# Attention probabilities turned in place, an output bank per unit, and a new order of the work

## The chip, the cores and the metric

The kernel runs on one core of a Trainium2 chip. The metric is the device time of one execution in microseconds (us). Three runs of the kernel before gave 2599.71 us as their median (2597.64 to 2602.36). About 0.2% of that, some 5 us, is what a measurement of this kernel can tell from no change.

Engines are named as the profile names them: PE (the matrix engine; PEld its weight loads), DVE, ACT and POOL (the three others that compute), SP (which issues the DMAs). PE's results land in PSUM, which has eight banks of 512 fp32 columns; everything else lies in SBUF, on 128 partitions.

## What is computed

One encoder layer over a short context (2 batches, 77 tokens, 512 features) and one decoder layer over x (2 batches, 2048 tokens), all in fp32. The decoder layer attends causally to itself, then to the encoder's output, and ends in a feed-forward network of width 2048:

```python
causal = jnp.where(jnp.arange(Tt)[None, :] > jnp.arange(Tt)[:, None], -jnp.inf, 0.0)
sb = _rel_bias(dec_rel_self, Tt, Tt) + causal[None]
y = tgt
yn = _ln(y, dec_n1_s, dec_n1_b)
y = y + _mha(yn, yn, dec_sa_in_w, dec_sa_in_b, dec_sa_out_w, dec_sa_out_b, sb)
y = y + _mha(_ln(y, dec_n2_s, dec_n2_b), memory, ...)
h = _ln(y, dec_n3_s, dec_n3_b)
y = y + (jax.nn.relu(h @ dec_ff1_w.T + dec_ff1_b) @ dec_ff2_w.T + dec_ff2_b)
```

with, inside `_mha` (16 heads of 32 features):

```python
scores = jnp.einsum('bhqd,bhkd->bhqk', q, k) / jnp.sqrt(hd) + bias[None]
attn = jax.nn.softmax(scores, axis=-1)
out = jnp.einsum('bhqk,bhkd->bhqd', attn, v)
```

## The kernel before

**The self-attention in units.** It is cut into 128 units. A unit (b, m, g, t) is one batch, one block of 128 queries (the t-th of four in the m-th of four blocks of 512 tokens) and one group g of four heads. It has `size = 4*m + t + 1` blocks of 128 keys, from 1 to 16. A unit goes through four steps:

- `scores`: for up to four key blocks at a time, four matmuls (one per head, 32 rows of the array each) into four banks. DVE brings the banks into `pp` while it takes their maximum; the last two key blocks get the bias and the causal mask on the way.
- the exps: one ACT instruction per head over all of the unit's key blocks, in place in `pp`, with the row's sum beside it.
- `turn`: for two key blocks at a time, 16 transposes of 64 rows each into two banks, and two copies of 512 columns out of them, by ACT or DVE, into `pts`.
- `values`: per key block four matmuls (32 columns of the array each) that take the turned blocks and add up in one bank.

**Places before.** `pp` has two halves, one for even and one for odd units. `pts` holds eight turned blocks and is handed out as a pool (`turned_places`). The bank of `values` is held by the four units t of one (b, m, g) and copied out once, 512 columns wide, after the fourth.

**Tile shapes on PE.** The steps use the array in four shapes (rows x columns): 64x128 for the turns, 128x32 for the values and the projections of q, k, v and of the output, 32x128 for the scores, 128x128 for the feed-forward network. The names in the trace tell them apart: `psum<-ident,pp` is a turn, `psum<-pts,vv` values, `psum<-kT,q` scores, `psum<-nT,wqk`, `psum<-wbig,nT` and `psum<-wbig,oT` projections. The trace shows each fp32 matmul as two instructions, and a transpose as one.

**What sets the order.** The program's operations are first recorded (`Tape`) as tasks, with the tasks that each depends on. `Tape.plan` then sets the order by walking through time with its own estimates of durations: each task has a key (the unit's number plus an offset by kind), and a table `PLAN` gives, for every four units, the offsets, how far PE may run ahead of the lowest open key (`window`), and how much a task is preferred that keeps PE's tile shape (`stay`). A task starts only where its banks and places are free. It also decides whether ACT or DVE makes a copy. Every engine then runs its instructions in that fixed order and waits on semaphores. SP's queue of DMAs is in the same order.

**Around it.** The encoder is computed in between the first units. In the middle of the attention POOL prepares sums of the weights of the feed-forward network (`w2_sums`, `w2_store`, `w1_sums`, `w1_store`), which go to DRAM (`w_d` in the trace). From 1544 us on the cross-attention and the feed-forward network run. Every recorded instruction carries the line of the recorder, L457 of the profile, so groups are told apart by their tiles.

Of the kernel before, what the change touches and what calls it, by code (L numbers as in the profile page):

```python
# [12 lines left out]
F32 = mybir.dt.float32  # L13
# [58 lines left out]
def phase_of(window, hold, flex, stay, first, wide, look, pause, weights):  # L72
# [744 lines left out]
def tile_encoder_decoder(ctx: ExitStack, tc: tile.TileContext, ins, out):  # L817
# [102 lines left out]
    with (  # L920
# [205 lines left out]
        def probabilities(n):  # L1126
            w = (units[n][1] + 1) * MB
            at = END - HC * w if n % 2 else 0
            return [pp[:, at + r * w : at + (r + 1) * w] for r in range(HC)]
# [1360 lines left out]
```

## Time and profile before

| | before |
|---|---|
| runs | 2602.36, 2597.64, 2599.71 us |
| profiled execution, first to last instruction | 2600.6 us; the profile gives no other time for it, and it lies among the three runs |
| PE busy | 2574.9 us |
| self-attention: up to the last `values` | 1544 us; PE busy 1524.86, DVE 1217.09, ACT 1097.99 |
| cross-attention and feed-forward: the rest | 1057 us; PE busy 1050.01, DVE 601.20, ACT 413.20 |
| granted clock of PE, mean | 0.998 |

How to read it: "busy" is the time in which at least one instruction of an engine is under way. Matmuls overlap in PE's pipeline, so a row of n equal matmuls takes far less than n times the duration of one. In the timeline, the start of a row to the start of the next is what the row cost.

### The profile page before, as it was taken

To read this page: it belongs to the slowest core of one execution; us is meant where nothing else is said; L and a number is where in the kernel's file an instruction comes from. 1 tells how busy PE (TensorE), PEld (TensorE's weight loads), DVE (VectorE), ACT (ScalarE), POOL (GpSimd) and SP (SyncE) were. 2 spreads that over 40 slices of the span, in tenths; PEclk is the share of its full clock that TensorE was granted. 3 is DMA by queue.
4 is the path that set the end of the run, shared out by engine and by line. 5 is a ranking of instruction groups with operands and counts; after the bars stand their busy time and mean duration, and the time that the engine had idled before them with its cause. 6 is when DMAs were issued, how large, how long until landed. Compare 5 with 4: busy or idle time off the path is not lost.

```text
span 2600.6 us, 84216 instructions
## 1 busy us (share of the span) xinstructions
PE 2574.9 (99%) x35494; PEld 1803.0 (69%) x35494; DVE 1818.3 (70%) x5243; ACT 1511.2 (58%) x2898; POOL 823.9 (32%) x757
## 2 busy tenths in 40 slices
PE   9999999999999999999999999999999999999999
PEld 4556555555555455555555677989898989999998
DVE  5766688788887787888788874747474746474744
ACT  4665578777877576678787874433425353434431
POOL 1200152000001011202000023938474757566546
PEclk9999999999999999999999999999999999999999
DMA  8323383111116222513112043646556655554566
GB/s 222 119 79 108 108 243 109 51 43 30 50 33 153 81 63 67 160 55 128 31 47 63 29 148 113 183 139 190 159 171 175 181 158 170 171 161 153 159 199 223
DMA packets 252716, 320.32 MB, mean 123 GB/s; under 512 B 29568, under 2 KB 142512, under 8 KB 252210
## 3 DMA queue, kind: packets, MB, share of 16 engines
q1 hardware_dynamic: 252338, 314.93, 40.7%
q8 instruction: 279, 4.57, 0.7%
q14 instruction: 99, 0.81, 0.1%
HBM read 274.91 MB, written 39.95 MB: 121 GB/s over the span
## 4 chain that ended last, share of the span: by engine, by line
PE 64%; ACT 1%; DVE 1%; issue 1%; DMA 0%; POOL 0%; POOLq 0%; ACTq 0%; DVEq 0%
PE psum L457 64%; ACT pp L457 0%; DVE pp L457 0%; ACT pts L457 0%; DMA pp<-w_d 0%; DVE pts L457 0%; DVE nT L457 0%; ACT nT L457 0%; DVE bnst L457 0%; POOLq L2486 0%; POOL vv L457 0%; DVE oT L457 0%; POOL crs L457 0%; ACT xt L457 0%; DVE vv L457 0%
## 5 line engine op out<-in xcount | busy, mean ns | idle before, releaser
L457 ACT ACTIVATE pp<-pp,nm 128x128 f32<-128x128 f32 (+15 forms) x512 | 612.9, 1204 | 141.0 <-DVE nm L457 140.5
L457 DVE TENSOR_SCALAR_CACHE_REDUCE pp<-psum 128x512 f32<-128x512 f32 (+3 forms) x1024 | 561.7, 590 | 124.2 <-PE psum L457 118.7
L457 ACT COPY pts<-psum 128x512 f32<-128x512 f32 (+2 forms) x789 | 404.6, 575 | 229.9 <-PE psum L457 191.4
L457 PEld LDWEIGHTS psum<-ident,pp 64*128 64x128 f32 (+1 forms) x8904 | 314.9, 139 | 182.7 <-issue 63.1
L457 PE MATMUL psum<-ident,pp 64*128 64x64 f32 (+1 forms) x8904 | 367.4, 227 | 5.8 <-DVE kT L457 1.5
L457 PE MATMUL psum<-pp 128*128 128x128 f32 (+4 forms) x3012 | 359.3, 281 | 0.3 <-DMA pp<-w_d 0.3
L457 PEld LDWEIGHTS psum<-pp 128*128 128x128 f32 (+3 forms) x3012 | 341.2, 189 | 15.6 <-DVE nm L457 1.6
L457 POOL TENSOR_TENSOR pp<-pp 128x512 f32<-128x512 f32 (+2 forms) x203 | 278.8, 1385 | 198.1 <-DVE pp L457 98.2
L457 PE MATMUL psum<-kT,q 32*128 32x512 f32 (+3 forms) x2560 | 334.4, 575 | 1.3 <-ACT nT L457 1.0
L457 DVE COPY pts<-psum 128x512 f32<-128x512 f32 (+2 forms) x475 | 288.5, 646 | 54.1 <-PE psum L457 51.0
L457 PE MATMUL psum<-pts,vv 128*32 128x128 f32 x8704 | 314.7, 276 | 4.7 <-ACT nT L457 2.8
L457 PEld LDWEIGHTS psum<-pts,vv 128*32 128x32 f32 x8704 | 220.9, 109 | 104.5 <-issue 70.2
L457 PE MATMUL psum<-vv,pp 128*128 128x256 f32 (+1 forms) x1072 | 254.1, 390 | 0.0
L457 PE MATMUL psum<-nT,wqk 128*32 128x512 f32 x2048 | 240.2, 595 | 2.5 <-DMA wqk<-in_dec_sa_in_wT_dram 1.3
L457 PEld LDWEIGHTS psum<-vv,pp 128*128 128x128 f32 (+1 forms) x1072 | 199.4, 188 | 39.3 <-issue 11.3
L457 DVE CUSTOM_DVE_ANT_0 pp<-psum,bias 128x256 f32<-128x256 f32 (+1 forms) x512 | 196.5, 411 | 25.7 <-PE psum L457 21.0
L457 DVE TENSOR_TENSOR oT<-psum,oT 128x256 f32<-128x256 f32 (+2 forms) x260 | 108.0, 425 | 122.7 <-PE psum L457 107.8
L457 PEld LDWEIGHTS psum<-kT,q 32*128 32x128 f32 x2560 | 108.3, 183 | 111.3 <-issue 45.2
L457 POOL TENSOR_TENSOR rstd<-rstd,mhalf 128x1 f32<-128x1 f32 x32 | 18.4, 576 | 506.5 <-DVE rstd L457 476.2
L457 PE MATMUL psum<-nT,pp 128*128 128x256 f32 x768 | 177.1, 382 | 0.0
L457 DVE TENSOR_TENSOR kT<-kT,psum 128x512 f32<-128x512 f32 x96 | 65.2, 682 | 139.4 <-PE psum L457 136.6
L457 PEld LDWEIGHTS psum<-nT,pp 128*128 128x128 f32 x768 | 143.6, 190 | 20.1 <-issue 0.6
(152 smaller groups left out, 3215.2 us busy)
## 6 DMA issues: line engine op xcount, KB each, us to landing
pp<-w_d SPq DMA_DIRECT2D x520, 256.0 KB, 2.9
pp<-in_dec_ff_wT_dram SPq DMA_DIRECT2D x112, 256.0 KB, 2.9
wqk<-in_dec_sa_in_wT_dram SPq DMA_DIRECT2D x64, 256.0 KB, 2.9
bias<-tzg SPq DMA_DIRECT2D x128, 128.0 KB, 3.3
wbig<-in_dec_sa_in_wT_dram SPq DMA_DIRECT2D x8, 1024.0 KB, 7.3
vv<-in_enc_ff_wT_dram SPq DMA_DIRECT2D x8, 1024.0 KB, 5.6
wbig<-in_dec_sa_out_wT_dram SPq DMA_DIRECT2D x8, 1024.0 KB, 5.9
vv<-y SPq DMA_DIRECT2D x32, 256.0 KB, 3.9
```

The lines of the kernel that those rows point to most:

```text
L457: getattr(getattr(self.nc, engine), op)(*map(real, a), **{n: real(v) for n, v in k.items()})
```

## The change

- **In place.** `pts` and its pool are gone. `pp` becomes a ring of 40 blocks, each a key block with its four heads side by side (2048 columns of one head per row become a step of 512 from key block to key block). A table `spots` gives each unit its blocks: fixed places for m = 0, 1, 2 and a ring for m = 3, where a unit may lie in two parts. `turn` copies the turned blocks back over the blocks that it read.
- **The exps** of a unit in two parts are two instructions per head, and a small DVE addition joins their sums.
- **An output bank per unit.** `values` takes a bank for each unit and copies it out, 128 columns wide, at the unit's end.
- **Other places.** What the cross-attention kept in `pts` is now at the end of `pp` (`tail`). The sums for the feed-forward network's second weights use the rear of `kT` and `vv`; their stores to DRAM are cut in another way (56 in place of 44).
- **New order.** Most of the attention's rows of `PLAN` have other numbers, and the order comes out otherwise. The matmuls and transposes are the same in number and shape.

```diff
@@ PLAN, one of 37 rows
-    (6.9, 2.5, 323, (0.463, 0.15, 0.337, 0.322), (-2.08, -0.5, 0, 1.75, -0.98, 0.33, -0.6, -0.5, -0.14, 0.42, -0.28),
+    (8.717, 1.874, 18, (0.835, 0.643, 0.759, 0.291), (-2.73, 0.328, 0, 0.919, 0.22, -0.017, -1.211, -1.071, -0.585, -0.499, -1.449),
...
-        pp = ac.tile([P, 2 * HC * T], F32, name="pp")
+        RING = 40
+        pp = ac.tile([P, RING * HC * P], F32, name="pp")
         END = 2 * HC * T
+        blocks_of_p = pp.rearrange("p (k r q) -> p k r q", r=HC, q=P)
...
-        pts_all = ac.tile([P, 8, HC * P], F32, name="pts")
...
-        banks, turned_places = Places(psum), Places(pts_all)
+        banks = Places(psum)
...
         def probabilities(n):
-            w = (units[n][1] + 1) * MB
-            at = END - HC * w if n % 2 else 0
-            return [pp[:, at + r * w : at + (r + 1) * w] for r in range(HC)]
+            size = units[n][1] * TB + units[n][3] + 1
+            at, first = spots[n]
+            parts = [(0, at, first)] + ([(first, 0, size - first)] if first < size else [])
+            return [(k, blocks_of_p[:, at : at + n]) for k, at, n in parts]
...
+        PLACES = ((0, 28, 32, 36), (0, 32, 24), (28, 0, 16))
...
+        for b, m, g, t in units:
+            size = m * TB + t + 1
+            if m < NMB - 1:
+                spot, at = (PLACES[m][(g * TB + t) % len(PLACES[m])], size), 0
+            else:
+                first = min(size, (RING - at) // TB * TB)
+                spot = (at, first) if first else (0, size)
+                at = sum(spot) if spot[1] == size else size - first
...
-                def run(p=p, nm=nm, to=to):
-                    nc.scalar.activation(p, p, AF.Exp, bias=nm, accum_out=to)
+                def run(r=r, nm=nm, to=to):
+                    parts = st["p"]
+                    for x, (_, p) in enumerate(parts):
+                        p = p[:, :, r]
+                        if x:
+                            to = st["more"][:, r : r + 1]
+                        nc.scalar.activation(p, p, AF.Exp, bias=nm, accum_out=to)
+                    if r == HC - 1 and len(parts) > 1:
+                        to = sums_of[b, m, g][:, t]
+                        nc.vector.tensor_tensor(to, to, st["more"], ALU.add)
...
         def turn(n, k0, kn):
-            pts = turned_places.take(kn)
+            place = part_of_p(n, k0, kn).rearrange("p k r q -> p (k r) q")
             two = [bank(), bank()]
...
-                        nc.tensor.transpose(two[a][:, ts(x, HALF)], src[at], ident[at, at])
...
+                        nc.tensor.transpose(two[a][:, ts(x, HALF)], place[rows, x], ident[rows, rows])
+            for a in range(2):
+                src = two[a][:, : HC * kn * HALF]
+                copy(place[:, :, ts(a, HALF)], src.rearrange("p (x q) -> p x q", q=HALF))
...
         def values(n, k0, kn):
...
-            if (b, m, g) not in held:
-                held[b, m, g] = bank()
...
+            if n not in held:
+                held[n] = bank()
+            if t == 0 and k0 == 0:
+                ots[b, m, g] = in_turn("oT", oT_all)
+            ot = held[n][:, :P]
...
-            if t == TB - 1 and k == i:
-                o = ots[b, m, g] = in_turn("oT", oT_all)
-                copy(o, got_bank)
+            if k == i:
+                copy(ots[b, m, g][:, ts(t, P)], ot)
...
-        for c, k in enumerate((0, 2, 4, 10)):
-            light[u + k + 2].append(lambda c=c: w2_store(c, 1))
-            late[u + k + 1].append(lambda c=c: w2_store(c, 0))
-        for c, k in enumerate((0, 2, 4, 10)):
+        for c, k in enumerate((0, 3, 6, 9)):
             light[u + k].append(lambda c=c: w2_sums(c))
+            for i, zs in enumerate(ranges):
+                light[u + k + 1 + i].append(lambda c=c, zs=zs: w2_store(c, *zs))
...
-        for t in nc.tasks[mark_loads:]:
-            if any(s.places is turned_places for s in t.slots):
-                t.before.add(behind)
```

**How the order moves.** Below, a row is a stretch of equal instructions on one engine; "x16" is their number in the program. Counted over all of PE's rows, the tile shape changes 1323 times before and 990 times after. Stretches without a change of shape go from 399 to 214 for the turns' shape (64x128), from 480 to 384 for that of the values and projections (128x32), from 349 to 297 for that of the scores (32x128), and stay at 96 for 128x128. The longest stretch of transposes goes from 80 to 152; stretches of more than 80 go from none to 42.

PE, the end of the second batch's attention, before: from the last unit's last scores (`kT,q`) to the first of its turns (`ident,pp`), with values (`pts,vv`), turns of the unit ahead and an output projection (`wbig,oT`) between them.

```order
L457 MATMUL psum<-kT,q_132 128x512 x4
L457 MATMUL psum<-ident,pp 128x64 x64
L457 MATMUL psum<-pts,vv 32x128 x16
L457 MATMUL psum<-ident,pp 128x64 x32
L457 MATMUL psum<-pts,vv 32x128 x16
L457 MATMUL psum<-ident,pp 128x64 x24
L457 MATMUL psum<-pts,vv 32x128 x16
L457 MATMUL psum<-wbig,oT 32x512 x8
L457 MATMUL psum<-pts,vv 32x128 x12
L457 MATMUL psum<-ident,pp 128x64 x64
```

PE, the same place after (the values now read `pp`).

```order
L457 MATMUL psum<-kT,q_131 128x512 x4
L457 MATMUL psum<-pp,vv 32x128 x16
L457 MATMUL psum<-wbig,oT 32x512 x16
L457 MATMUL psum<-ident,pp 128x64 x48
L457 MATMUL psum<-pp,vv 32x128 x8
L457 MATMUL psum<-ident,pp 128x64 x32
L457 MATMUL psum<-pp,vv 32x128 x8
L457 MATMUL psum<-ident,pp 128x64 x16
L457 MATMUL psum<-pp,vv 32x128 x8
L457 MATMUL psum<-ident,pp 128x64 x24
L457 MATMUL psum<-pp,vv 32x128 x36
L457 MATMUL psum<-ident,pp 128x64 x128
```

The last unit's 128 transposes, which stood in three pieces with values between them, now stand in one; other work stands between its last scores and its first turn as before, in another mixture.

PE, some units earlier in the same block of queries, before: turns, values and scores alternate.

```order
L457 MATMUL psum<-ident,pp 128x64 x16
L457 MATMUL psum<-kT,q_132 128x512 x4
L457 MATMUL psum<-ident,pp 128x64 x16
L457 MATMUL psum<-pts,vv 32x128 x16
L457 MATMUL psum<-ident,pp 128x64 x32
L457 MATMUL psum<-kT,q_132 128x256 x4
L457 MATMUL psum<-pts,vv 32x128 x8
L457 MATMUL psum<-ident,pp 128x64 x16
L457 MATMUL psum<-kT,q_132 128x512 x4
```

PE, there after.

```order
L457 MATMUL psum<-kT,q_131 128x256 x4
L457 MATMUL psum<-pp,vv 32x128 x4
L457 MATMUL psum<-ident,pp 128x64 x128
L457 MATMUL psum<-kT,q_131 128x512 x4
L457 MATMUL psum<-pp,vv 32x128 x32
L457 MATMUL psum<-kT,q_131 128x512 x4
L457 MATMUL psum<-pp,vv 32x128 x16
L457 MATMUL psum<-kT,q_131 128x512 x4
L457 MATMUL psum<-pp,vv 32x128 x16
```

All turns of a unit now stand in one stretch, and its scores and values alternate without turns between them.

ACT, the last units, before: exps (`pp,sums<-pp,nm`) and copies of turned blocks (`pts<-psum`).

```order
L457 COPY pts<-psum 128x8x64 x2
L457 ACTIVATE pp,sums_145<-pp,nm_139 128x1792
L457 COPY pts<-psum 128x8x64 x8
L457 ACTIVATE pp,sums_145<-pp,nm_140 128x1920
L457 COPY pts<-psum 128x8x64 x4
L457 ACTIVATE pp,sums_145<-pp,nm_140 128x1920 x3
L457 COPY pts<-psum 128x8x64 x4
L457 ACTIVATE pp,sums_145<-pp,nm_141 128x2048 x4
L457 COPY pts<-psum 128x8x64 x8
L457 COPY oT<-psum 128x512
```

ACT, there after (the copies go back to `pp`, and `oT` is filled unit by unit).

```order
L457 COPY pp<-psum 128x8x64 x8
L457 ACTIVATE pp,sums_144<-pp,nm_139 128x15x128 x2
L457 COPY pp<-psum 128x8x64 x2
L457 ACTIVATE pp,sums_144<-pp,nm_139 128x15x128 x2
L457 ACTIVATE pp,sums_144<-pp,nm_140 128x16x128 x2
L457 COPY pp<-psum 128x8x64 x3
L457 ACTIVATE pp,sums_144<-pp,nm_140 128x16x128 x2
L457 COPY pp<-psum 128x4x64
L457 COPY oT<-psum 128x128
L457 COPY pp<-psum 128x8x64 x9
L457 COPY oT<-psum 128x128
```

Over the whole program ACT makes 600 of the copies of 8x64 in place of 650 and DVE 424 in place of 374, and the eight wrapped units give ACT 32 more exps.

More of the change, by code (lines that the diff above doesn't have):

```diff
@@ L1829, in tile_encoder_decoder @@
         pr = oflat[:, : H * S]
-        kTc_places = [turned_places.take() for b in range(B)]
+        tail = [pp[:, END + k * D : END + (k + 1) * D] for k in range(8)]
+        kTc_places = tail[:2]
         kTcs = [a[:, : NC * S].rearrange("p (c k) -> p c k", k=S) for a in kTc_places]
-        turned_pairs = [turned_places.take(2) for _ in range(2)]
+        turned_pairs = [pp[:, END + 2 * k * D : END + 2 * (k + 1) * D].rearrange("p (g q) -> p g q", g=2) for k in (1, 2)]
         w_q, vcs, qT = {}, [], []
@@ L1866, in early_loads @@
                 load_w_q(n)
-            w_q["S2"] = turned_places.take()
+            w_q["S2"] = tail[6]
         def last_loads():
@@ L2236, in q_product @@
                 nc.scalar.activation(dst[:, f], got[:, f], AF.Identity, bias=q_bias[:, g : g + 1], scale=SCALE)
-        xt_ring, xt_turn = [turned_places.take()], [0]
+        xt_ring, xt_turn = [tail[7]], [0]
         def next_xt():
@@ L2393, in tile_encoder_decoder @@
                 turn(n, k, kn)
-            if n == end - 2:
-                nc.key = "load", n + 1, 0
-                feed(len(w_ring))
             if n + 1 < end:
@@ L2401, in tile_encoder_decoder @@
                 values(n, k, kn)
+            if n == end - 2:
+                nc.key = "load", n + 1, 0
+                feed(len(w_ring))
         last = [t for t in nc.tasks if t.ways[0][0] == "PE"][-1]
-        behind = [t for t in nc.tasks if t.kind[:2] == ("turn", end - 1) and t.ways[0][0] == "PE"][BEHIND]
-        mark_loads = len(nc.tasks)
         nc.key = "load", end, 0
@@ L2408, in tile_encoder_decoder @@
         for t in (2, 3):
-            residual_load(*blocks[-1], t, turned_places.take())
+            residual_load(*blocks[-1], t, tail[t])
         late_loads()
```

99 lines of the change are left out of this document (48 added, 51 removed), and 144 rows, old and new, of the table PLAN.

## Prediction

> **What bounds the kernel now.** I read the page's busy lines first, then the windows of the two stages.
>
> ```profile
> span 2600.6 us, 84216 instructions
> PE 2574.9 (99%) x35494; PEld 1803.0 (69%) x35494; DVE 1818.3 (70%) x5243; ACT 1511.2 (58%) x2898; POOL 823.9 (32%) x757
> ```
>
> ```profile
> 0.00:1544.00 1544.00, 1524.86 (x26766) 854.81 (x26766) 1217.09 (x4131) 1097.99 (x2021) 189.96 (x208) 1.00 0.31 90
> 1544.00:2601.00 1057.00, 1050.01 (x8736) 948.15 (x8728) 601.20 (x1112) 413.20 (x877) 633.95 (x550) 1.00 0.57 172
> ```
>
> The columns after the length are busy us (and instructions) of PE, PEld, DVE, ACT, POOL, then PE's clock, DMA share and GB/s. PE is the bound in both stages: in the attention it stands idle for 1544.00 - 1524.86 = 19.1 us, while DVE is busy for 79% and ACT for 71%. Waits explain little, so the time is in what PE does. There the timeline is read from the start of a row to the start of the next. First the turns (64*128). The trace counts a transpose once and a matmul twice, the order each once: x16 of values here is x8 there.
>
> ```profile
> 1000.32 0.46 PE L457 MATMUL psum<-ident,pp 64*128 64x64 f32 x8
> 1000.71 0.71 PE L457 MATMUL psum<-kT,q 32*128 32x256 f32 x8
> 1001.35 0.64 PE L457 MATMUL psum<-pts,vv 128*32 128x128 f32 x16
> 1001.93 2.10 PE L457 MATMUL psum<-ident,pp 64*128 64x64 f32 x48
> 1003.81 0.47 PE L457 MATMUL psum<-ident,xt 64*128 64x64 f32 x8
> ```
>
> ```profile
> 1532.32 1.90 PE L457 MATMUL psum<-wbig,oT 128*32 128x512 f32 x16
> 1534.04 0.84 PE L457 MATMUL psum<-pts,vv 128*32 128x128 f32 x24
> 1534.81 0.56 PE L457 MATMUL psum<-ident,pp 64*128 64x64 f32 x10
> 1535.76 2.24 PE L457 MATMUL psum<-ident,pp 64*128 64x64 f32 x54 [0.39 <-issue]
> 1537.93 1.08 PE L457 MATMUL psum<-pts,vv 128*32 128x128 f32 x32
> 1538.94 1.22 PE L457 MATMUL psum<-ident,pp 64*128 64x64 f32 x32
> 1540.09 1.08 PE L457 MATMUL psum<-pts,vv 128*32 128x128 f32 x32
> 1541.10 1.22 PE L457 MATMUL psum<-ident,pp 64*128 64x64 f32 x32
> 1542.25 1.95 PE L457 MATMUL psum<-pts,vv 128*32 128x128 f32 x64
> 1544.13 7.17 PE L457 MATMUL psum<-nT,pp 128*128 128x256 f32 x32
> ```
>
> Eight transposes cost 1000.71 - 1000.32 = 0.39 us, 32 cost 1.15. So 24 more cost 0.76: 0.25 for eight, and 0.39 - 0.25 = **0.14 us** is paid once a stretch, however long it is. The values: 32 cost 1541.10 - 1540.09 = 1.01, 64 cost 1.88; 32 more cost 0.87, and again 1.01 - 0.87 = **0.14 us** is paid once. This is the price of one stretch, between a change of the array's shape and the next; it lies within PE's busy time, so no wait shows it.
>
> **The change, part by part.** *Fewer changes of shape.* The matmuls are the same, and over the whole program the order has 1323 changes before and 990 after. By the kind of stretch: turns 399 to 214, 185 fewer, at 0.14 = 25.9 us. Values and projections 480 to 384, 96 fewer, at 0.14 = 13.4 us; for the projections the nearest row is 1532.32, where 16 cost 1.72 with values of the same shape behind them. Scores 349 to 297, 52 fewer; no row shows two scores in one stretch without a wait, so the bounds are 0 and 0.14 each, 0 to 7.3 us. I take 0: a longer stretch of scores also fills more banks at once. Sum: **-39.3 us**.
>
> *Waits of PE.* Two things pull apart. First the exps' lead. In the place shown of the order PE has, between the last unit's last scores and its first turn, before: 64 transposes (2.14 at the prices above), 32 (1.15) and 24 (0.89), three lots of values (1.01 each), a projection (1.72) and 12 values (0.77), 9.7 us. It did not suffice: the row at 1534.81 breaks off after 10 transposes, and 64 of them took 1537.93 - 1534.81 = 3.12 where 2.14 was due. After, by the same prices: values and projection in one stretch 4.45, turns of 48, 32, 16, 24 (1.64, 1.15, 0.64, 0.89), three lots of 8 values (0.58 each, as at 1001.35) and 36 values (2.10), 12.6 us. What has to fit in is four exps, one behind the other:
>
> ```profile
> L457 ACT ACTIVATE pp<-pp,nm 128x2048 f32<-128x2048 f32 x32 | 64.1, 2018 | 7.2 <-DVE nm L457 7.2
> L457 ACT ACTIVATION_READ_ACCUMULATOR pp<-pp,nm 128x1 f32 x512 | 101.1, 198 | 0.0
> ```
>
> 4 x (2.02 + 0.20) = 8.9 us, behind DVE's readings of the scores. So 2.9 us more of cover, where before fell short by about one. At best all 19.1 us of idle go: -19.
>
> Second, the emptying of the banks. A turn of 16 transposes fills two banks in 0.50 us; they are emptied by two copies:
>
> ```profile
> L457 ACT COPY pts<-psum 128x512 f32<-128x512 f32 x650 | 345.2, 593 | 169.8 <-PE psum L457 131.7 <-issue 17.9 <-DVE pp L457 9.0
> L457 DVE COPY pts<-psum 128x512 f32<-128x512 f32 x374 | 240.9, 682 | 27.3 <-PE psum L457 24.5 <-issue 1.2 <-ACT pts L457 0.2
> ```
>
> With both engines free a turn is emptied in about 0.64, a little slower than it is made. Eight banks swallow four or five turns; before, no stretch had over 80 transposes (five turns), after, 42 have. The nearest rows are the longest shown: 48 transposes at 1001.93 cost 1.88 where 6 x 0.25 + 0.05 (no change of shape behind them, so less than the 0.14) were due, 0.33 too many; the 64 above 0.98. Some 0.6 for each of the 42 is +25 us. If the 70 turns beyond a stretch's fifth only pay 0.64 - 0.50, it is +10. Bounds -19 and +25; I take the middle, **+3**.
>
> *What ACT and DVE get besides.* 50 copies go from ACT to DVE, 50 x 0.682 = 34 us more there and 50 x 0.593 = 30 less on ACT. The output goes out in 184 copies of 128 columns, of which 128 are new, in place of 32 of 512:
>
> ```profile
> L457 ACT COPY oT<-psum 128x128 f32<-128x128 f32 x56 | 15.0, 267 | 176.7 <-PE psum L457 162.4 <-DVE cmv L457 9.2 <-issue 1.8
> L457 ACT COPY oT<-psum 128x512 f32<-128x512 f32 x25 | 14.7, 589 | 11.8 <-PE psum L457 11.7
> L457 DVE COPY oT<-psum 128x512 f32<-128x512 f32 x7 | 4.8, 689 | 4.0 <-PE psum L457 4.0
> L457 ACT ACTIVATE pp<-pp,nm 128x128 f32<-128x128 f32 x32 | 12.5, 395 | 16.1 <-DVE nm L457 16.1
> ```
>
> 82 on ACT at 0.267 less 25 at 0.589, +7; 46 on DVE at no more than 0.3 less 7 at 0.689, +9. The 32 split exps cost a start each, at most 0.395 + 0.198 (as for one key block), +19 on ACT. The steps of 512 in the exps and of 64 in the copies I price at nothing: copies into 64-wide pieces take 593 and 682 ns, whole ones 589 and 689. So in a stage of some 1505 us ACT comes to about 1094 (73%) and DVE to 1217 + 43 = 1260 (84%). Off PE's path: their idle time covers it, on DVE only 245 us. Were it not covered, the 43 us would come on top, which is more than the gain.
>
> *Other places and stores.* POOL's additions are as many as before; SP issues 12 more stores of sums.
>
> ```profile
> SPq L457 <- PE psum L457: 1506.9, 692, 52.6
> SPq L457 <- POOL pp L457: 60.5, 14, 23.6
> POOL xr L457 <- DMA xr<-in_x_dram: 365.9, 22, 136.0
> ```
>
> Behind a store that waits for POOL, SP holds the next loads; it did so for 60.5 us in all without a mark on PE, as SP mostly waits for PE itself. Cost 0; with the cover gone, one late weight load of 2.9 us:
>
> ```profile
> wqk<-in_dec_sa_in_wT_dram SPq DMA_DIRECT2D x64, 256.0 KB, 2.9
> PE psum L457 <- DMA wqk<-in_dec_sa_in_wT_dram: 1.3, 1, 1.3
> ```
>
> The second stage has the same stretches; I count its 1057 us as they are. The loads of the residual into `tail` now come behind the last values, where they came behind the last turn: 0 to 3 us, covered by 32 matmuls of 7.17 us (row at 1544.13).
>
> *Sum* against the profiled execution: 2600.6 - 39.3 + 3 = 2564.3. Its span is 0.9 us over the runs' median of 2599.7. Forecast **2564 us**, with 2535 (-7.3 for the scores, -19) and 2586 (+25) as its own bounds.
>
> **The rivals.**
>
> *The copies become the bound* (the other side). If ACT is in exps while a unit's turns stand in one stretch, DVE empties both banks alone: 2 x 0.682 = 1.36 a turn against 0.50, 0.86 of waiting for each of the 70 turns beyond a fifth, +61 us: 2600.6 - 39.3 + 61 = 2622, slower. It decides from a mean wait of 39.3 / 70 = 0.56 us a turn. For it: DVE at 84%, and the waits in the long rows shown. Against it: the order's rows on ACT after have 8 and 9 copies in a row, without exps between them. In the Trainium skill, "TensorEngine Tiling (Array Packing)", section "PSUM Bottleneck", warns that tiling speeds up the matrix engine but not the emptying of PSUM, and advises both engines for the copies; the rows above agree, with 0.64 against 0.50. Chance 0.06.
>
> *Half of it is lost so*: the same waits at 0.25 to 0.45 a turn, 18 to 31 us: 2579 to 2592, middle 2586. Chance 0.12.
>
> *The clock.* PE's clock fell to half twice:
>
> ```profile
> 463.46:466.87 3.41, 1.48 (x24) 0.59 (x24) 0.29 (x1) 1.94 (x5) 0.00 (x0) 1.00 0.00 0
> 466.87:470.28 3.41, 3.41 (x32) 1.23 (x24) 2.24 (x8) 3.41 (x5) 0.00 (x0) 0.50 0.02 5
> 1309.96:1313.37 3.41, 2.98 (x65) 2.45 (x64) 3.13 (x9) 2.42 (x5) 0.00 (x0) 1.00 0.02 5
> 1313.37:1316.79 3.42, 3.42 (x54) 1.60 (x48) 2.97 (x13) 0.82 (x2) 0.00 (x0) 1.00 0.00 0
> 1310.14 1.28 PE L457 MATMUL psum<-ident,pp 64*128 64x64 f32 x33
> 1312.96 2.70 PE L457 MATMUL psum<-kT,q 32*128 32x256 f32 x16
> ```
>
> After a window with 1.48 us of work, the next 3.41 us ran at 0.50. If long transposes counted as idle, the 20 stretches of 112 and more (3.5 us each) would bring a half window each, 1.7 us lost: 20 x 1.7 = 34, 2600.6 - 39.3 + 3 + 34 = 2598, no change. Against it: the window at 1309.96 had nothing but transposes from 1310.14 to 1312.96, and the next stayed at 1.00. In the Trainium skill, "TensorE: Matmul & The Clock Gate", section "Part 4: PE-mode transpose", says that transposes don't count as busy for the clock gate; by that rule the window would have been idle, and the trace disagrees. Chance 0.03.
>
> *It doesn't do what it says*: a stretch's 0.14 is a wait on semaphores that moves along. Then nothing is saved, 2600.6 + 3 = 2604. Against it: 0.14 comes out alike for two kinds, at 1000 and at 1540 us. Chance 0.02.
>
> **How the numbers follow.** 0.77 for 2564, then 0.12, 0.06, 0.03 and 0.02. Below 2550 I leave 0.1, above 2588 0.1 (the upper part of the half case, and the others): range 2550 to 2588. 0.2% is 5 us here. Faster takes 0.77 and the half case, 0.89; same takes the clock and the case without effect, 0.05; slower 0.06.
>
> **What would show it.** In the profile after: PE's changes of shape at 990 and 0.14 a stretch; PE busy near 2540; transposes of 128 at 4.1 us and not 5; the attention's end near 1508 us; DVE at about 84% before it; no new clock of 0.50. Wrong if PE's idle time in the attention is over 40 us, or the long rows of turns take over 0.5 us more than 0.25 for eight.

## The result, and the profile after

The changed kernel takes **2568.06 us** (median of four runs, 2563.66 to 2570.30) where the kernel before takes 2598.91: a ratio of **0.9878, 95% interval 0.9864 to 0.9892**. The forecast was 2564. The profiled execution spans 2565.1 us, 35.5 less than the one of before; the medians are 30.9 apart, the rest is which execution was profiled. The page's busy lines of the changed kernel:

```profile
span 2565.1 us, 84358 instructions
PE 2533.8 (99%) x35494; PEld 1810.7 (71%) x35494; DVE 1840.2 (72%) x5324; ACT 1504.4 (59%) x2985; POOL 820.7 (32%) x757
```

Its two stages as windows (length, busy us and instructions of PE, PEld, DVE, ACT, POOL, PE's clock, DMA share, GB/s):

```profile
0.00:1508.00 1508.00, 1485.16 (x26786) 864.27 (x26787) 1240.46 (x4213) 1091.52 (x2110) 193.82 (x211) 1.00 0.32 92
1508.00:2565.00 1057.00, 1048.59 (x8709) 946.41 (x8707) 599.78 (x1111) 412.86 (x875) 626.93 (x547) 1.00 0.57 171
```

PE's busy time fell by 41.1 us, with the same 35494 matmuls. In the attention PE stands idle for 1508.00 - 1485.16 = 22.8 us (19.1 before). So the gain is again inside PE's busy time, and a little was lost to waits. PE's timeline in the changed kernel, with long stretches:

```profile
1055.00 0.71 PE L457 MATMUL psum<-ident,pp 64*128 64x64 f32 x16
1055.64 1.96 PE L457 MATMUL psum<-pp,vv 128*32 128x128 f32 x64
...
1133.29 2.00 PE L457 MATMUL psum<-kT,q 32*128 32x512 f32 x16
1135.22 2.35 PE L457 MATMUL psum<-nT,wqk 128*32 128x512 f32 x20
...
1284.28 1.08 PE L457 MATMUL psum<-pp,vv 128*32 128x128 f32 x32
1285.29 1.47 PE L457 MATMUL psum<-ident,pp 64*128 64x64 f32 x40
1286.69 1.52 PE L457 MATMUL psum<-pp,vv 128*32 128x128 f32 x48
1288.14 1.14 PE L457 MATMUL psum<-kT,q 32*128 32x512 f32 x8
1289.21 0.86 PE L457 MATMUL psum<-pp,vv 128*32 128x128 f32 x24
...
1295.67 3.83 PE L457 MATMUL psum<-ident,pp 64*128 64x64 f32 x112
1299.42 0.84 PE L457 MATMUL psum<-pp,vv 128*32 128x128 f32 x21
```

From start to start, 16 transposes cost 0.64 and 40 cost 1.40: 24 more for 0.76, so 0.25 for eight and 0.14 once, as before. 32 values cost 1.01 and 48 cost 1.45: 0.13 once. New is the row at 1133.29: two score tasks in one stretch cost 1.93, while a single one (1288.14) costs 1.07. Two stretches would be 2.14, so a stretch of scores costs **0.21 us** once. Not every row is so clean: of the 124 stretches of one such task 115 cost under 1.15 us (median 1.07), and of the 23 of two tasks 11 cost 1.93, but their mean is 2.02.

Adding up all rows of PE's trace by the array's shape, from the start of each stretch to the start of the next (us; in brackets the stretches), gives the balance:

| | turns 64x128 | values, projections 128x32 | scores 32x128 | 128x128 |
|---|---|---|---|---|
| before | 398.4 (399) | 842.0 (480) | 355.1 (349) | 997.1 (96) |
| changed | 384.0 (214) | 830.9 (384) | 340.3 (297) | 1001.9 (96) |
| difference | -14.4 | -11.1 | -14.8 | +4.8 |
| stretches saved, by 0.14, 0.14, 0.21 | -25.9 | -13.4 | -10.9 | 0 |
| rest | +11.5 | +2.3 | -3.9 | +4.8 |

The saved stretches are worth 50.2 us, and 14.7 were given back: 10.8 up to the last values (the attention ends at 1504.7 us for 1544.1), and 3.9 behind them (1060.4 us to the end of the program for 1056.5; the rest of the 4.8 of the 128x128 shape lies earlier). Each sum is that of one profiled execution, so a difference of 1 us in it says little. The experiments ask whether the price of a stretch is real, whether order and places need each other, and where the 14.7 went.

### The profile page after: what moved, and what is told of

The parts are those of the page before. It is cut to its first block, busy times and chain, and to the rows that moved or that the text cites. A ratio compares the mean times of both kernels' runs of the same rounds, so it can differ in the third digit from the quotient of the medians.

```text
span 2565.1 us, 84358 instructions
## 1 busy us (share of the span) xinstructions
PE 2533.8 (99%) x35494; PEld 1810.7 (71%) x35494; DVE 1840.2 (72%) x5324; ACT 1504.4 (59%) x2985; POOL 820.7 (32%) x757
## 5 line engine op out<-in xcount | busy, mean ns | idle before, releaser
L457 ACT ACTIVATE pp<-pp,nm 128x384 f32<-128x384 f32 (+15 forms) x544 | 620.8, 1155 | 114.6 <-DVE nm L457 112.0
L457 ACT COPY pp<-psum 128x512 f32<-128x512 f32 (+3 forms) x783 | 384.5, 578 | 195.6 <-PE psum L457 147.3
L457 PEld LDWEIGHTS psum<-pp 128*128 128x128 f32 (+3 forms) x3068 | 352.7, 189 | 14.8 <-issue 3.2
L457 PE MATMUL psum<-pp,vv 128*32 128x128 f32 (+1 forms) x10240 | 355.0, 282 | 5.5 <-issue 2.5
L457 PEld LDWEIGHTS psum<-pp,vv 128*32 128x32 f32 x10240 | 273.9, 110 | 122.5 <-issue 87.2
L457 PE MATMUL psum<-ident,pp 64*128 64x64 f32 (+1 forms) x8976 | 345.9, 227 | 10.9 <-ACT nT L457 6.0
L457 DVE COPY pp<-psum 128x512 f32<-128x512 f32 (+3 forms) x513 | 309.3, 653 | 31.0 <-PE psum L457 25.9
L457 PE MATMUL psum<-kT,q 32*128 32x512 f32 (+3 forms) x2560 | 318.9, 569 | 1.5 <-DVE oT L457 0.9
L457 POOL TENSOR_TENSOR pp<-pp 128x512 f32<-128x512 f32 (+2 forms) x167 | 231.6, 1397 | 116.8 <-DVE pp L457 98.4
L457 PEld LDWEIGHTS psum<-vv,pp 128*128 128x128 f32 (+1 forms) x1072 | 200.7, 189 | 39.5 <-issue 11.1
L457 POOL TENSOR_TENSOR xr<-xr,row_dec_sa_out_b 128x512 f32<-128x512 f32 x30 | 38.4, 1282 | 510.8 <-DMA xr<-in_x_dram 510.8
L457 ACT COPY oT<-psum 128x128 f32<-128x128 f32 x138 | 36.7, 268 | 235.4 <-PE psum L457 218.9
```

Of the source, the lines that this page charges most:

```text
L457: getattr(getattr(self.nc, engine), op)(*map(real, a), **{n: real(v) for n, v in k.items()})
```

## The experiments

Each time is a median beside runs of the kernel before (2598.4 to 2601.8 in the four sets, so times of different sets compare to some 3 us only), with the ratio to before and its 95% interval. "Stretches" are turns, values and projections, scores; the next column is the time by shape in the same order, then that of 128x128.

| kernel | us | ratio | stretches | us by shape |
|---|---|---|---|---|
| before | 2598.91 | 1 | 399, 480, 349 | 398.4, 842.0, 355.1; 997.1 |
| changed | 2568.06 | 0.9878 (0.9864 to 0.9892) | 214, 384, 297 | 384.0, 830.9, 340.3; 1001.9 |
| e1, old table | 2616.75 | 1.0067 (1.0054 to 1.0079) | 356, 466, 343 | 407.0, 847.8, 353.7; 998.7 |
| e2, old places | 2663.99 | 1.0250 (1.0236 to 1.0264) | 363, 489, 342 | 439.5, 842.9, 368.6; 999.3 |
| e3, bank for four | 2636.27 | 1.0143 (1.0129 to 1.0156) | 287, 467, 344 | 417.2, 847.2, 359.0; 1000.4 |
| e4, split | 2579.39 | 0.9919 (0.9905 to 0.9933) | 261, 431, 297 | 393.6, 836.2, 342.8; 999.7 |
| e6, half copies | 2555.83 | 0.9829 (0.9815 to 0.9842) | 214, 384, 297 | 375.1, 829.1, 341.3; 1002.5 |
| e7, one-bank reads | 2550.70 | 0.9806 (0.9793 to 0.9820) | 214, 384, 297 | 379.0, 826.9, 338.1; 997.8 |
| e8, scores split | 2590.80 | 0.9968 (0.9955 to 0.9980) | 214, 419, 332 | 382.2, 836.0, 363.1; 999.1 |
| e9, last values | 2565.82 | 0.9867 (0.9851 to 0.9882) | 215, 385, 297 | 385.3, 831.5, 341.6; 997.4 |
| e10, e7 and e9 | 2553.48 | 0.9814 (0.9801 to 0.9828) | 215, 385, 297 | 379.7, 829.3, 337.0; 996.5 |
| e11, before, one-bank reads | 2590.49 | 0.9959 (0.9947 to 0.9972) | 399, 480, 349 | 398.9, 836.6, 346.5; 998.7 |
| e12, all one-bank | 2563.28 | 0.9849 (0.9836 to 0.9863) | 214, 384, 297 | 384.3, 829.3, 341.2; 999.2 |
| e13, before, half copies | 2589.76 | 0.9957 (0.9943 to 0.9970) | 399, 480, 349 | 390.3, 836.7, 351.2; 997.9 |

### Order without places, places without order, and the output bank

```diff
 e1: the changed kernel
-PLAN = [...]   # the new rows
+PLAN = [...]   # the rows of before
 e2: the kernel before
-PLAN = [...]   # the rows of before
+PLAN = [...]   # the new rows
 e3: the changed kernel, values
-            if n not in held:
-                held[n] = bank()
+            if (b, m, g) not in held:
+                held[b, m, g] = bank()
...
-            if k == i:
-                copy(ots[b, m, g][:, ts(t, P)], ot)
+            if t == TB - 1 and k == i:
+                o = ots[b, m, g] = in_turn("oT", oT_all)
+                copy(o, got_bank)
```

> The changed code (probabilities turned back in place, an output bank per unit) with the planner's old table of numbers, so that only the order differs from the changed kernel. Stretches of PE between two array shapes: turns 356, values and projections 466, scores 343 (changed kernel 214, 384, 297; before 399, 480, 349). Theory 1, a price per stretch (0.14 us for turns and values, 0.21 us for scores): from the changed kernel's 2568.1 us it is (142 + 82) x 0.14 + 46 x 0.21 = 41 us more, 2609; reckoned from before's 2598.9 it is (43 + 14) x 0.14 + 6 x 0.21 = 9 less, 2590; the two ends differ by the waits, so 2590 to 2609, and by shape of the array the turns take about 20 us more than in the changed kernel, the scores about 10 more. Rival, the gain comes from the code (copies in place, smaller output copies): 2566 to 2575. Rival, the gain comes from waits that the order avoids and a stretch costs nothing: the time may be anywhere, but time by array shape differs only where PE is shown idle.

> The kernel before (turned blocks in eight places of their own, one output bank for four units) with the new table of the planner. Stretches: turns 363, values and projections 489, scores 342. Theory 1, a price per stretch: from before 36 x 0.14 - 9 x 0.14 + 7 x 0.21 = 5 us less, 2594; reckoned from the changed kernel 149 x 0.14 + 105 x 0.14 + 45 x 0.21 = 45 more, 2613; so 2590 to 2613, because eight places and a bank for four units do not let long stretches form. Rival, the table alone brings the gain: 2566 to 2575.

> The changed kernel, but the four units of a group share one output bank that is copied out 512 wide once, as before; the planner then finds another order. Stretches: turns 287, values and projections 467, scores 344. Theory 1: 73 x 0.14 + 83 x 0.14 + 47 x 0.21 = 32 us more than the changed kernel, 2600 (waits of -10 to +10 on it: 2590 to 2610). Rival, the output bank is a detail and the gain lies in the places of the turned blocks: 2566 to 2575. Rival, the many small output copies cost: below 2568.

None of the three is as fast as the kernel before, and all three lie above the range that I expected (2609, 2613 and 2610 at its upper end). The new code in the old table's order is 0.7% slower, the new table on the old code 2.5% slower, the new table with one output bank for four units 1.4% slower. The rivals that gave the gain to one part alone (2566 to 2575, or below 2568) are out. With these two tables the gain needs the three together: the places and the bank per unit allow long stretches to form, and the table was made for them. A table made anew for the new places with one bank for four units was not tried. Reckoned from the changed kernel, the price of the stretches explains e1 in size (41 us of 48.7) and by shape: turns +23.0 for 19.9 reckoned, values +16.9 for 11.5, scores +13.4 for 9.7. Reckoned from the kernel before it does not: e1 has 63 stretches fewer, worth 9 us, and is 18 us slower, so it holds some 27 us of waits more than before (in its attention PE's granted clock was 0.50 for 23.9 us, for 6.8 before). In e2 and e3 it is 45 and 32 us of 96 and 68; the rest is waits. PE's waits of e2 (us in total, times, longest), where the changed kernel has 3.2 and 2.0 in the same two rows:

```profile
PE psum L457 <- ACT pp L457: 14.5, 18, 1.7
PE psum L457 <- DVE pp L457: 10.1, 22, 1.1
```

An order made for other places makes PE wait for blocks of `pp` that are not ready.

### The price of a stretch by itself

```diff
+SPLIT = ("turn", "turn", "value", "value"), ("value", "value", "turn", "turn")   # e4
+SPLIT = [("score", "score", k, k) ...] + [(k, k, "score", "score") ...]   # e8, k = turn, value
+def split(order, most):
...
+    for x in range(2, len(pe) - 1):
+        a0, a, v, v2 = pe[x - 2], pe[x - 1], pe[x], pe[x + 1]
...
+        if v.came > a.at - 100:
+            continue
...
+        order[i : j + 1] = [v] + between
...
         order = nc.plan(PLAN, STEP)
+        order = split(order, SPLITS)
```

> The changed kernel with the same tasks, places and banks; in 47 places of PE's order, where two tasks of turns meet two of values (or the other way round) and the later one's data are long there, the two middle ones change places. Nothing else differs, so PE gets 94 stretches more (turns 214 to 261, values 384 to 431) and no work. Theory 1, 0.14 us a stretch whichever order makes it: 94 x 0.14 = 13 us more, up to 6 less where a shorter stretch of turns gives its copies time: 7 to 13 us above the changed kernel's 2568, 2575 to 2581; by array shape turns +2 to +7, values +6 to +7. Rival, what the changed kernel gained was waits and a stretch costs nothing: 2562 to 2569.

> The changed kernel, where in 35 places of PE's order two tasks of scores meet two of turns or values: the two middle ones change places. Stretches of scores go from 297 to 332, of values from 384 to 419, nothing else differs. Theory 1, a score stretch costs 0.21 us: 35 x 0.21 + 35 x 0.14 = 12 us above the changed kernel's 2568, 2580, and by array shape scores +7, values +5. Rival, the prediction's choice that a score stretch costs nothing: 35 x 0.14 = 5, 2573, scores +0 to +1.

In e4 only 47 pairs of neighbouring tasks change places, and it costs 11.3 us (13.2 reckoned), outside the rival's 2562 to 2569. Turns and values lose 14.9 us, against 13.2 by the price (turns +9.6 for 6.6, values +5.3 for 6.6, both outside what I expected by shape), and the intervals of the two ratios lie apart. So a stretch costs its price whichever order makes it; it isn't a wait that moves along.

e8 is less clean. Values rise by 5.1 for 4.9 reckoned, but scores by 22.8 for 7.4. e8's timeline shows why (PEld is the weight load of PE):

```profile
457.10 0.65 PE L457 MATMUL psum<-pp,vv 128*32 128x128 f32 x16
457.67 1.62 PE L457 MATMUL psum<-kT,q 32*128 32x512 f32 x8
457.81 0.29 DVE L457 COPY oT<-psum 128x128 f32<-128x128 f32 x1 [1.62 <-PE psum L457]
458.16 0.30 PEld L457 LDWEIGHTS psum<-kT,q 32*128 32x128 f32 x6 [0.19 <-DVE oT L457]
```

The value task that was moved between is the last of its unit. Its bank is copied out at 457.81, and the scores behind it take that bank and stand until 458.16; the row costs 1.55 and not 1.07 (the next begins at 459.22). Of single stretches of scores 512 wide, 42 last over 1.15 us in e8 and 9 in the changed kernel, most of the new ones by 0.4 to 0.5 too long; the two that I followed have this cause. Both expectations of e8 are missed. Less what single tasks take over 1.07 each (20.1 us in e8, 5.4 in the changed kernel) the scores rise by 8.1 for the 7.4 reckoned, so e8 fits the 0.21 once these waits are taken out; a score stretch that costs nothing fits neither e8 nor the rows above nor the sum of e1 (13.4 for 46 stretches, 0.29 each with waits).

### What PE waits for: the copies

```diff
+                if t.kind[0] == "turn" and t.engine in ("ACT", "DVE") and op in ("copy", "tensor_copy"):
+                    a = tuple(x[:, : x.shape[1] // 2] for x in a)
```

> The changed kernel in the very same order, but every copy of a turned block back from PSUM is half as wide: half of each turned block is left as it was, so the values are computed from blocks of which one half was not transposed. Stretches as in the changed kernel. It asks how much of the time PE waits for these copies. If the copies set the pace in the long stretches of turns (the first rival of the prediction), the turns take 365 us instead of 384 and the run is 10 to 20 us shorter, 2548 to 2558. If they are covered, as the prediction has it, and what waits are left come from other work: 0 to 4 us shorter, 2564 to 2568.

> The kernel before, in its own order, with every copy of a turned block half as wide (the places of the turned blocks are zeroed once at the start, which takes some us there, so the time is read by the shape of the array and not from the run): half of each turned block stays zero and the values are computed from that. In the changed kernel the same edit took 8.9 us off the time of the turns. Theory, most of these waits are new, made by its long stretches: here turns fall by 0 to 4 us, from 398.4 to 394 or more. Rival, the copies cost as much before: 8 to 10 us, 388 to 390.

Halving the copies in the changed kernel takes 12.2 us off the run and 8.9 off the turns: the run lies inside the rival's range (2548 to 2558), the turns about half way to its 365. So PE does wait for these copies. In the changed kernel the 42 stretches of over 80 transposes took 8.6 us over 0.253 for eight and 0.14 a stretch, and the 172 shorter ones 19.6; with half the copies 4.3 and 15.0 are left. That is far from the 61 us of the prediction's first rival. The Trainium skill, "TensorEngine Tiling (Array Packing)", section "PSUM Bottleneck", warns that copies out of PSUM may become the bottleneck; here they cost PE some 9 us and do not bound it. The same halving in the kernel before takes 8.1 off its turns: here my theory fell, waits for copies were there before any long stretch. Net, halving is worth 8.9 - 8.1 = **0.8 us** more after the change, which one execution each can't tell from nothing.

### What PE waits for: reads across banks

The changed kernel's longest stall of PE, at 411 us (the rows of PE, of ACT's reads of the norm and one of DVE; the last two rows are windows):

```profile
411.08 0.27 PE L457 MATMUL psum<-ident,pp 64*128 64x64 f32 x1
411.22 0.46 ACT L457 ACTIVATE nT<-psum,vecs 128x128 f32<-128x128 f32 x1
411.73 0.72 PE L457 MATMUL psum<-ident,pp 64*128 64x64 f32 x16 [0.38 <-ACT nT L457]
412.48 0.46 ACT L457 ACTIVATE nT<-psum,vecs 128x128 f32<-128x128 f32 x1 [0.80 <-PE psum L457]
413.04 0.69 DVE L457 TENSOR_TENSOR xr<-psum,xr 128x512 f32<-128x512 f32 x1 [1.74 <-ACT nT L457]
413.76 0.46 ACT L457 ACTIVATE nT<-psum,vecs 128x128 f32<-128x128 f32 x1 [0.83 <-DVE xr L457]
414.28 0.71 PE L457 MATMUL psum<-ident,pp 64*128 64x64 f32 x15 [1.83 <-ACT nT L457]
415.02 0.46 ACT L457 ACTIVATE nT<-psum,vecs 128x128 f32<-128x128 f32 x1 [0.80 <-PE psum L457]
415.54 1.38 PE L457 MATMUL psum<-ident,pp 64*128 64x64 f32 x32 [0.55 <-ACT nT L457]
...
413.01:416.42 3.41, 1.59 (x43) 1.46 (x45) 2.10 (x5) 1.85 (x5) 0.82 (x2) 1.00 0.20 77
416.42:419.83 3.41, 3.41 (x44) 2.08 (x43) 3.14 (x12) 2.05 (x5) 1.16 (x1) 0.50 0.26 79
```

ACT reads the turned norm in four columns, each from two banks at once; PE turns probabilities into other banks, and DVE reads a projection from another. They have no data in common, yet they wait for each other in turn. The plan in the kernel's code gives the banks: the norm lies in 1 and 6, the turn at 411.08 writes 0 and 5 in turn, the next one 7 and 2, and DVE reads 4. The first transpose of each of the two turns, into 0 or 7, goes ahead (x1, and the last of x16); the second, into a bank between 1 and 6, waits for ACT. After 1.59 us of work in 3.41, PE's clock is at 0.50 for the next 3.41. Where no two neighbouring banks are free, the norm's and the division's two banks are any two, and the read has a step over the banks between: 41 of 192 such reads in the changed kernel, 47 in the one before.

```diff
+                apart = [x for x in a if isinstance(x, View) and x.slot.n == 2 and x.slot.at
+                         and abs(x.slot.at[1] - x.slot.at[0]) > 1]   # e12: neighbours too
+                if engine in ("scalar", "vector") and apart:
+                    halves = [tuple(y[:, h] if len(getattr(y, "shape", ())) > 2 else y for y in map(real, a)) for h in range(2)]
...
+                for h in halves:
+                    getattr(getattr(self.nc, engine), op)(*h, **{n: real(v) for n, v in k.items()})
```

> The changed kernel in the same order on PE; the 41 reads of two PSUM banks that are not neighbours (the norm's columns, the division) are each made as two reads of one bank, 41 small instructions more on ACT and DVE. Theory, a read that spans two banks makes the work on the banks between them wait, which is where PE stood longest (3.6 us at 411, 2.3 at 1013): those waits and the half clock after them go, 4 to 8 us less than the changed kernel, 2560 to 2564. Rival, PE waits there for ACT's own load and the banks between do not matter: 2568 to 2571, the stalls at 411 and 1013 stand.

> The kernel before, with each read of two banks that are not neighbours (47 of them) made as two reads of one bank, in the order of before. It asks whether the change brought the waits on the banks between, or whether they were there already. Theory, they were there: PE waits 4.9 us for ACT's norm columns and fell to half clock twice (1.7 us each); 4 to 12 us less than before's 2599, 2587 to 2595, so that the change itself is worth some 40 us once both are freed of them. Rival, only long stretches of turns run into them: 2596 to 2600.

> The changed kernel in the same order with all 192 reads of two banks made as reads of one bank, the 151 of neighbouring banks too: over 200 small instructions more on ACT and DVE than the changed kernel. Theory, only a read that spans other banks does harm: as with the 41 alone, 2549 to 2554, no more gain. Rival, any read of two banks holds PE up: 2545 or less. If the small instructions on ACT reach the path: over 2556.

e7 is the fastest kernel of this study but one that ties with it (e10): **2550.70 us, 17.4 less than the changed kernel**, over twice what I expected, though ACT and DVE have 59 instructions more (41 reads, and 18 copies of the cross-attention out of such slots that were halved as well, 6 of them in the attention's time). Around the same place its timeline reads:

```profile
409.22 2.44 ACT L463 ACTIVATE nT<-psum,vecs 128x64 f32<-128x64 f32 x8
409.25 1.73 PE L463 MATMUL psum<-ident,pp 64*128 64x64 f32 x48
411.71 0.72 PE L463 MATMUL psum<-ident,pp 64*128 64x64 f32 x16 [0.73 <-ACT nT L463]
```

Eight reads in one go beside 48 transposes, in place of four reads over 4.3 us. PE's waits for ACT's norm columns, in the changed kernel and in e7:

```profile
PE psum L457 <- ACT nT L457: 6.9, 8, 2.2
```

```profile
PE psum L463 <- ACT nT L463: 2.1, 4, 0.7
```

All four stretches at half clock of the changed kernel (from 13.65, 416.42, 1017.16 and 1515.51, 3.41 us each; about 1.7 lost each, 7 in all, of the 15.3 that the span fell) are gone; only the one at the program's end is left. Two of the four can't be laid to these reads, as by the plan the banks of the first are filled at 239.9 us and those of the last at 1461.6. At 13 us e7 waits as before (0.60 and 0.62 us for the norm, in the changed kernel 0.64 and 0.62), and behind the attention it still waits 1.6 us in two pieces (1.9), but no window fell to half clock. So 3.4 of the 15.3 are luck in where the windows fell.

e11 does the same to the kernel before: 11.3 us by the medians with intervals apart, and both its half clocks (466.87, 1023.24) go. So the waits were there already, and the rival is out. In spans they cost the one before 11.9, and the changed kernel 15.3, or 11.9 without the two half clocks that weren't theirs; up to the last values alone it is 13.5 and 13.2. The change made them no dearer. In e12 the 151 reads of neighbours are halved too (the 18 copies are left whole): nothing more is gained, and some 12 us of the 17.4 are lost again. So it isn't the splitting that helps; that the banks between do the harm is read from the stall at 411 and its banks. There I had expected no more than 2554: 133 more instructions than e7, and PE waits 4.6 us for ACT's `pp` (0.8 in e7), with half clocks at 13.22 and 282.88. With this loss beside it, e12 can't exclude a small cost of the neighbours' reads.

### The handover to the second stage

The end of the changed kernel's attention and what follows. The rows up to 1500.45 are the last unit's last exp, its 128 transposes and ACT's copies of them (DVE's are left out, as other rows are); the row at 1501.09 has its values, all in one stretch; the SPq row is the queue of loads; the last two rows are windows:

```profile
1493.13 1.99 ACT L457 ACTIVATE pp<-pp,nm 128x2048 f32<-128x2048 f32 x1
1495.94 4.01 PE L457 MATMUL psum<-ident,pp 64*128 64x64 f32 x112
1496.74 4.32 ACT L457 COPY pp<-psum 128x512 f32<-128x512 f32 x8 [0.40 <-PE psum L457]
1500.45 0.71 PE L457 MATMUL psum<-ident,pp 64*128 64x64 f32 x16 [0.51 <-ACT pp L457]
1501.09 3.70 PE L457 MATMUL psum<-pp,vv 128*32 128x128 f32 x128
1501.58 4.25 SPq L457 DMA_DIRECT2D vv<-y  x8
1504.72 1.99 PE L457 MATMUL psum<-nT,pp 128*128 128x256 f32 x8
1506.65 0.46 PE L457 MATMUL psum<-ident,rirows 64*128 64x64 f32 x8
1507.04 5.45 PE L457 MATMUL psum<-nT,pp 128*128 128x256 f32 x24
1511.01 0.69 DVE L457 BATCH_NORM_STATS2 bnst<-vv 128x6 f32<-128x512 f32 x1 [3.09 <-DMA vv<-y]
1514.00 0.66 PE L457 MATMUL psum<-ident,xt 128*128 128x128 f32 x4 [1.51 <-ACT xt L457]
...
1512.10:1515.51 3.41, 1.55 (x11) 0.93 (x10) 3.20 (x11) 1.62 (x2) 3.04 (x6) 1.00 1.07 356
1515.51:1518.92 3.41, 3.41 (x10) 2.34 (x8) 0.82 (x2) 3.16 (x9) 3.41 (x5) 0.50 0.67 247
```

`y` is loaded into blocks of `vv` that the last values have read. Before, these values came in three lots, and this row

```profile
1538.41 3.91 SPq L457 DMA_DIRECT2D vv<-y  x8
```

stands 5.7 us ahead of their end (1544.13); in one stretch of 128 the blocks come free late, and the row stands 3.1 us ahead (1504.72). The 7.8 us of PE's work from 1504.72 on no longer cover load and norm: 1.51 us idle, then half a clock.

```diff
+def last_values(order, n):
...
+    for t, at in zip(turns[5:], LAST_BANKS):   # (2, 1), (7, 4), (6, 2)
+        for s, i in zip(t.slots, at):
+            s.at = [i]
+    rest = [t for t in order if t not in values[:4]]
+    x = rest.index(turns[5])
+    return rest[:x] + values[:4] + rest[x:]
```

> The changed kernel, but of the last unit's eight value tasks the first four run ahead of the last three tasks of turns (with other banks for these three), so that the first blocks of the values come free about 2 us earlier; two stretches more. In the changed kernel the last values are one stretch of 128 matmuls, the loads of y into their places start 3.1 us before its end, and PE then waits 1.5 and 0.35 us for the norm of y and falls to half clock. Theory, the merged stretch delays these loads: the wait goes to under 0.5 us and the half clock with it, 2 to 4 us less after the attention, 2564 to 2566. Rival, the loads are as late whatever releases them (their queue is full): within 1 us of 2568, PE's wait for xt stays near 1.5.

> One-bank reads in place of the reads that span other banks, together with the last unit's values brought forward. Alone they made 2550.7 and 2565.8 where the changed kernel has 2568. With one-bank reads PE still waits 1.6 us for the norm of y behind the attention, but its clock no longer falls there. Theory, that wait goes and nothing else changes: 1 to 2 us less, 2548.5 to 2550. Rival, the waits only move to the next load: 2550 to 2552.

In e9 the loads stand 7.5 us ahead of the last value's end, both waits for `xt` and the half clock at 1515 are gone, and from the last values to the end it takes 1056.4 us, as before the change (1056.5, in the changed kernel 1060.4). So the 3.9 of the second stage are found. The run gains 2.2 us only, and the intervals overlap: the moved values now wait themselves, and end 2.6 us later (1507.3).

```profile
1501.13 1.08 PE L457 MATMUL psum<-pp,vv 128*32 128x128 f32 x32 [0.73 <-DVE pp L457]
1506.62 0.77 PE L457 MATMUL psum<-pp,vv 128*32 128x128 f32 x17 [0.93 <-issue]
```

Beside one-bank reads (e10) nothing is gained: 2553.48 is above the 2550 to 2552 of its rival, and its interval takes in e7's ratio. The best kernel is e7.

## Why the prediction was right, and where not

- **What bounds it.** PE's changes of shape are the time, at 0.14 us a stretch for turns, values and projections. Right: the rows after give the same 0.14, and e4 gets it back by splitting stretches, near enough in sum (14.9 for 13.2). The rival "it doesn't do what it says" is out.
- **Turns -25.9, values -13.4.** The counts held (990 changes of shape). The shapes fell by 14.4 and 11.1 with their waits.
- **Scores 0.** The wrong choice within "0 to 0.14 each", and the bound was too low: 0.21 by the clean rows, 10.9 us for the 52. The 14.8 measured hold waits too: with both kernels freed of reads across banks (e11 and e7) the scores are 8.4 apart, 0.16 a stretch. My reason, that longer stretches fill more banks at once, holds in part only: the 23 of two tasks lose 0.09 of the 0.21 in the mean.
- **Waits +3.** Mis-sized, though inside its -19 to +25: 10.8 us were given back in the attention. The best case of -19 did not come, as PE's idle time there rose from 19.1 to 22.8. The exps' lead sufficed: the last exp of the last unit is over at 1495.12, ahead of its transposes at 1495.94. In the kernel before, too, the break at 1534.81 can't be laid to the exps, as the last one's sum was read by 1534.98 and PE went on at 1535.76. The emptying of banks came, but at a third of its price: the 42 stretches of over 80 transposes took 8.6 us too much, 0.2 each where 0.6 (+25) was the bound and +10 the milder figure. Two rows stand out, at 1444.94 and 1495.94, where 128 transposes took 5.09 and 5.16 for the 4.14 due: in the first DVE still reads scores up to 1447.19 and ACT empties alone, in the second PE breaks off for 0.51 until a copy of ACT is through. The 172 shorter stretches took 19.6 too much, all 399 of before 16.7; why these waits did not become fewer with the stretches is open. Reads across banks, which the prediction never named, cost at most 13.2 us here and 13.5 before, so they are no part of what was given back.
- **Second stage 0.** Wrong: +3.9. The step was "covered by 32 matmuls of 7.17 us". The cover was the same, but it was spent on `y`, whose loads the merged values held back.
- **DVE and ACT.** Forecast at 1260 and 1094 us before the end of the attention, measured 1240 and 1092. "Off PE's path" holds in the sum and not at the two rows just named, where PE waits for copies.
- **The sum.** -39.3 + 3 against -35.5: two errors of opposite sign, 11 us too little saved by scores and 12 too little for waits and handover. That 2564 came so near the 2568 is luck in this part. With both kernels freed of reads across banks (e7 against e11) the spans are 38.9 apart and the medians 39.8, near the bare sum of 39.3; that agreement too hides 8.4 for the scores and 9.7 that turns and values fell short of their price (19.9 for 25.9, 9.7 for 13.4).
- **The rivals.** The copies as the bound: the 112 at 1295.67 took 3.75 where 14 x 0.25 + 0.14 = 3.64 was due, and PE's idle time in the attention was 22.8, not over 40. But of the 20 stretches of 112 and more, five took over 0.5 us more than 0.25 for eight and 0.14, which the prediction had named as a sign of being wrong: there are waits in places, not a bound. The clock on long transposes: none of the four half clocks follows a long stretch without a wait, and the stretches of 3.5 us and more ran at 1.00. The Trainium skill, "TensorE: Matmul & The Clock Gate", section "Part 4: PE-mode transpose", says that a transpose "doesn't count as PE-busy the same way" for the clock; the runs disagree, as no half clock follows even 152 of them (4.95 us in one stretch). But the sign "no new clock of 0.50" failed: four in place of two, all behind waits of PE.
- **Signs.** PE busy 2533.8 for "near 2540"; the attention's end 1504.7 for 1508; transposes of 128 at 4.39 (median of six) for 4.1, two of them over 5; DVE 82% for 84%.

## What to carry to other kernels

Where PE is 99% busy, look at what a stretch costs from start to start for two lengths; the part that doesn't grow with the length is paid at each change of the array's shape, and the places of the operands decide how long stretches can be. A planner's numbers and the places that it plans for are one change: either half alone was slower than neither. When work is merged into longer stretches, list what waits for its first piece (loads into the places that it frees), and look for two engines that alternate in waiting without common data: freeing 41 strided reads over other buffers (and 18 copies) gained more here, 17.4 us, than halving every copy of a turned block, 12.2.

## What the runs showed of the hardware that I had not expected

- A stretch of scores (32x128, four heads side by side) costs 0.21 us once where nothing holds it up, not 0.14: 1.93 for two tasks in one, 2 x 1.07 apart.
- In this kernel a read of two PSUM banks that aren't neighbours keeps the banks between from PE, and PE's writes there keep the read back, 0.80 us each time at 411. The profile shows it as waits on semaphores; whether the chip itself would need them was not tried.
- A stall of PE of 1.5 to 2 us can cost about 1.7 more: after windows of 3.41 us with 1.59 and 1.55 us of PE's work, and before the change after one with 2.19 (1019.83), the next 3.41 us ran at 0.50. Whether it does depends on where the windows lie: 1.6 us of waits behind the attention brought none in e7.
